# Moving the first block's output projection behind its feed-forward stage, in a time-mix and GELU kernel

## The chip, the cores and the metric

The kernel runs on one core of a Trainium2 chip. The time of a run is the device time of that core in microseconds (us), from the start of the program to its end; the figure for a kernel is the median over runs. A profile of one execution stands beside it: its span runs from the first to the last instruction recorded, a little less than that execution's own time.

## The reference

The input x has 4 sequences of 1024 tokens with 512 channels. Each token is normalized, and the result goes into two branches whose outputs are added to x. The first is a time-mix: a key and a receptance product with 704 hidden units, a decaying running sum over time, and a projection back to 512 channels that is normalized again. The second is a feed-forward network (FFN) with 2048 hidden units, whose activations are rounded to 16 bits.

```python
xn = layernorm(x)
xx = shift(xn) - xn                      # the token before, minus the token
k = (xn + xx * mix_k) @ Wk.T             # 512 -> 704
r = (xn + xx * mix_r) @ Wr.T
state_t = state_{t-1} * exp(-exp(decay)) + relu(k_t)
a = layernorm((state * r) @ Wv.T) * gamma + beta      # 704 -> 512
D = gelu(f16(xn) @ W0.T + bias0).astype(f16)          # 512 -> 2048
E = (D @ W1.T + bias1).astype(f16)                    # 2048 -> 512
out = x + a + E
```

## The kernel before

**Blocks and stages.** The 4096 tokens are cut into 8 blocks of 512 (128 tokens x 4 make a block's token tiles). One loop runs over the blocks. For each block the tensor engine (PE) does, in this order in most blocks: the FFN (`ffn`), the output projection of the time-mix (`attention_out`, tiles po), and the key and receptance products of the next block (`attention`, tiles pk and pr). The 704 hidden units are five chunks of 128 and a half chunk of 64; the half chunk is computed by `half_chunk` (tiles pkr), which splits the PE's array into quarters of 64x64. Its sum `kr` is made on the vector engine (DVE, lines 438 and 439), its relu on the scalar engine (ACT, line 384), its running sum on DVE (line 386) and its product gh on DVE (line 442).

**Where the output projection stands.** In blocks 1 to 6, `attention_out` follows the FFN, and the next block's `half_chunk` is called from inside it (`amid`), right after the 64-row products of the projection (tile gh, line 470). In block 0 and in the last block (`within`), `attention_out` is put into the FFN at step n = 0, and the next block's half chunk then stands alone, behind its five full chunks.

**The FFN.** It has 16 chunks n of 128 hidden units. `up(n)` is eight products with W0, which is kept in a high and a low part (w0h, w0l)[...]; ACT applies the GELU (line 540), DVE casts the result to d (line 542). `down(n)` is eight products of d with the two parts of W1 (line 548). The order on PE is up(0), up(1), and then up(n + 2), down(n) for each n, so down(n) comes five eight-product groups after up(n), less at the end, where no further up stands between.

**Weights in block 0.** W0 and W1 arrive as plain 32-bit tiles `raw`, of which there are three buffers, shared by W0 (`load_w0`, 16 loads of 256 KB in four groups of four) and W1 (`load_w1`, 16 loads). Each is split: ACT copies the rounded high part (line 134), DVE subtracts to get the low part (line 135). A W1 chunk has one of three w1 buffers; in block 0 it is also stored to memory (w1d), from where the later blocks load both parts. up(0) to up(3) read W0's first group, up(12) to up(15) its last. In the kernel before, all four W0 groups are loaded before the FFN of block 0 is written down.

**What orders the work.** Each engine, and SyncE (SP), which issues nearly all DMAs, works through its own list in order. The lists are made ahead of time by a planner: the instruction written first in the program has the higher priority, and an instruction that is ready by the planner's own costs may fill a hole earlier. `tc.issue_after(ins)` puts the instructions in its block that run on the same engine as `ins` behind it in that engine's list. Buffers of one tag are taken in the order of the program. The layernorm of the next block (`next_norm`), its transposes (`transposed`, 16 on DVE, line 216) and its mixing (`mixed_inputs`, lines 349 to 367) are called inside the FFN, at n = 4 and, in block 0, n = 9; tile st6, with two buffers, is shared by the statistics of both layernorms.

Of the kernel before, what the change touches and what calls it, by code (L numbers as in the profile page):

```python
# [1 line left out]

# [9 lines left out]
AF = mybir.ActivationFunctionType  # L12
# [7 lines left out]
def time_mix_and_gelu_ffn(  # L20
# [26 lines left out]
    nc = tc.nc  # L47
# [5 lines left out]
    NC = C // P  # L53
# [79 lines left out]
    def split(hi, lo, raw):  # L133
        nc.scalar.copy(hi, raw)
        nc.vector.tensor_sub(lo, raw, hi.bitcast(F32))
# [4 lines left out]

    w1_dram = [dram.tile([P, 2, C], F32R, name=f"w1d_{n}") for n in range(NN)]

    def load_w0(g):
        for c in range(NC):
            raw = three.tile([P, W0G], F32, tag="raw", name=f"w0raw_{g}_{c}")
            cols = slice(g * W0G, (g + 1) * W0G)
            nc.sync.dma_start(raw, w0T[c * P : (c + 1) * P, cols])
            split(w0h[c][:, cols], w0l[c][:, cols], raw)

    def load_w1(i, n):  # L150
        if i == len(blocks) - 1 and n == NN - 1:

            parts = [
                three.tile([P, C], F32R, tag="raw", name=f"w1_{i}_{n}_{p}") for p in range(2)
            ]
            for p in range(2):
                nc.sync.dma_start(parts[p].bitcast(F32), w1_dram[n][:, p, :].bitcast(F32))
            return parts
        w1 = wide.tile([P, 2, C], F32R, tag="w1", name=f"w1_{i}_{n}", bufs=3)
        if i == 0:  # L160
            raw = three.tile([P, C], F32, tag="raw", name=f"w1raw_{n}")
            nc.sync.dma_start(raw, w1T[n * P : (n + 1) * P, :])
            split(w1[:, 0, :], w1[:, 1, :], raw)
            kept = nc.sync.dma_start(w1_dram[n].bitcast(F32), w1.bitcast(F32))
            if n == NN - 1:
                state["kept"] = kept
        else:
            nc.sync.dma_start(w1.bitcast(F32), w1_dram[n].bitcast(F32))
        return [w1[:, p, :] for p in range(2)]
# [206 lines left out]
    def attention(i, xk, pks=()):  # L376

        b, t0 = blocks[i]  # L380

        def states(h, hw, pk):
            rk = two.tile([P, TB], F32, tag="rk", name=f"rk_{i}_{h}", bufs=1)
            nc.scalar.activation(rk[:hw], pk, AF.Relu)  # L384
            st = two.tile([P, TB], F32, tag="st", name=f"st_{i}_{h}")
            nc.vector.tensor_tensor_scan(  # L386
                st[:hw],
                w_sb[:hw, h : h + 1].to_broadcast([hw, TB]),
                rk[:hw],
                0.0 if t0 == 0 else carry[:hw, h : h + 1],  # L390
                ALU.mult,
                ALU.add,
            )
            if t0 + TB < T:
                nc.gpsimd.tensor_copy(carry[:hw, h : h + 1], st[:hw, TB - 1 : TB])
            return st

        def full_chunks():
            g = one.tile([P, NF, TB], F32, tag="g", name=f"g_{i}")
            for h in range(NF):  # L400
                cols = slice(h * P, (h + 1) * P)
                if h < len(pks):
                    pk = pks[h]
                else:
                    pk = ps_mm.tile([P, TB], F32, tag="mm", name=f"pk_{i}_{h}")
                    for c in range(NC):
                        product(pk, wk_sb, cols, xk[:, c, :], c)
                st = states(h, P, pk)
                pr = ps_mm.tile([P, TB], F32, tag="mm", name=f"pr_{i}_{h}")
                for c in range(NC):  # L410
                    state["pr"] = product(pr, wr_sb, cols, xnT[:, c, 1:], c)
                nc.vector.tensor_mul(g[:, h, :], st, pr)  # L412
            return g

        def tokens(ap, odd):
            return ap.rearrange("p (s two t) -> p s two t", two=2, t=P)[:, :, odd, :]

        def half_chunk():
            gh = one.tile([P, NS // 2, P], F32, tag="gh", name=f"gh_{i}")


            sums = [ps_e.tile([P, TB], F32, tag="pe", name=f"pkr_{i}_{q}") for q in range(2)]
            for c in range(NC):
                for q, sum_ in enumerate(sums):
                    rows = slice(q * HF, (q + 1) * HF)
                    for out_, w, src in (
                        (sum_[:HF], wk_sb, xk[rows, c, :]),
                        (sum_[HF:], wr_sb, xnT[rows, c, 1:]),
                    ):
                        nc.tensor.matmul(  # L430
                            out_,
                            w[c][rows, H0:],
                            src,
                            start=(c == 0),
                            stop=(c == NC - 1),
                        )
            both = two.tile([P, TB], F32, tag="xx", name=f"kr_{i}")
            nc.vector.tensor_copy(both, sums[0])
            nc.vector.tensor_add(both, both, sums[1])  # L439
            st = states(NF, HF, both[:HF])  # L440
            for odd in range(2):
                nc.vector.tensor_mul(
                    gh[odd * HF : (odd + 1) * HF],
                    tokens(st[:HF], odd),
                    tokens(both[HF:], odd),
                )
            return gh

        return full_chunks, half_chunk
# [72 lines left out]
    def ffn(i, xf, between, state):  # L522
# [4 lines left out]
        def up(n):  # L527
            pd = ps_mm.tile([P, TB], F32, tag="mm", name=f"pd_{i}_{n}")
            cols = slice(n * P, (n + 1) * P)
            for c in range(NC):  # L530
                for w in (w0h, w0l):
                    nc.tensor.matmul(  # L532
                        pd,
                        w[c][:, cols],
                        xf[:, c, :],
                        start=(c == 0 and w is w0h),
                        stop=(c == NC - 1 and w is w0l),
                    )
            d16 = two.tile([P, TB], F16, tag="d16", name=f"d16_{i}_{n}")
            state["gelu"] = nc.scalar.activation(d16, pd, AF.Gelu, bias=b0_sb[:, n : n + 1])  # L540
            d = wide.tile([P, TB], F32R, tag="d", name=f"d_{i}_{n}", bufs=4)
            nc.vector.tensor_copy(d, d16)  # L542
            return d

        def down(n, s, d, w1, first=0, end=NN, sum_=None, cols=slice(0, C)):
# [27 lines left out]
        AHEAD = 2  # L573
        waiting = [(up(n), load_w1(i, n)) for n in range(AHEAD)]
        for n in range(NN):
            if n in between:
                between[n]()
            if n + AHEAD < NN:
                waiting.append((up(n + AHEAD), load_w1(i, n + AHEAD)))
            if n < NN - last:  # L580
                operands = waiting.pop(0)
                for s in range(NS):
                    down(n, s, *operands, end=NN - last if s in by_columns else NN)
# [19 lines left out]
    first_x16s, xk, pks = first_inputs(x_now, behind)  # L603

    full_chunks, half_chunk = attention(0, xk, pks)
    g = full_chunks()
    xf = ffn_input(0, first_x16s())
# [2 lines left out]
    for i in range(len(blocks)):  # L612
        more = i + 1 < len(blocks)
        if i == 0:
            for grp in range(N // W0G):
                load_w0(grp)
            behind.close()
            load_late_constants()
        if more:

            with tc.issue_after(state["kept"].ins) if i == 1 else nullcontext():
                x_now = load_x(i + 1)

        def out_stage():
            state["zs"] = attention_out(i, g, gh)

        def next_norm():
            with tc.issue_after(added.ins) if added else nullcontext():
                layernorm(i + 1, x_now)

        def next_inputs():
            transposed(x_now)
            state["mixed"] = mixed_inputs(i + 1, state["gelu"])

        within = i == 0 or not more
        added = state.get("added")
        between = {0: out_stage} if within else {}
        if more:
            between[4] = next_norm
            between[9 if i == 0 else 7] = next_inputs  # L640
        pe = ffn(i, xf, between, state)
        if more:
            x16s, xk = state["mixed"]
            e16s = [rounded(i, s, pe[s]) for s in range(NS)]
            xf = ffn_input(i + 1, x16s)
            full_chunks, half_chunk = attention(i + 1, xk)
            next_gh = []
            if within:
                zs = state["zs"]
            else:  # L650
                zs = attention_out(i, g, gh, lambda: next_gh.append(half_chunk()))
            for s in range(NS):
                finish(i, s, zs[s], e16s[s])
            g = full_chunks()
            gh = next_gh[0] if next_gh else half_chunk()
# [43 lines left out]
```

## Time and profile before

| quantity | value |
|---|---|
| median of 3 runs | 937.12 us (936.71 to 937.28) |
| profiled execution, its own time | 937.08 us |
| its span | 935.2 us |
| PE busy | 930.0 us, 99% |
| DVE busy | 501.6 us, 54% |
| ACT busy | 164.4 us, 18% |
| TensorE clock granted | 1.0 of full speed |

The profile's page has a row of busy shares for each engine, the chain of work that ended last, and the costliest groups of instructions. "PE" is the matmuls, "PEld" the loading of their stationary operand. A 32-bit product is recorded as two matmuls, a product of rounded operands as one; "pk L222 x8" is therefore one chunk of four products. Times in the chain are start and length in us, from the span's start.

### The profile page before, as it was taken

The numbers are of one execution on the slowest core, as the hardware profiler recorded it, in microseconds if no ns is written. First come the engines' busy times: TensorE is split into PE (matmuls) and PEld (weight loads), VectorE is DVE, ScalarE is ACT, GpSimd is POOL, SyncE is SP. The second block draws the span as 40 slices with busy tenths as digits, with TensorE's granted clock in tenths as the row PEclk, the third lists the DMA queues.
The fourth block names the chain that finished last, engine by engine and source line by source line (L and its number), as shares of the span: only waits on it lengthen the run. The fifth ranks groups of instructions, "written<-read, shape, count | busy, mean of one in ns | idle before, by whom it ended". The sixth has DMA issues, their size and how long they took to land.

```text
span 935.2 us, 9363 instructions
## 1 busy us (share of the span) xinstructions
PE 930.0 (99%) x3521; PEld 593.8 (63%) x3521; DVE 501.6 (54%) x878; ACT 164.4 (18%) x273; POOL 55.6 (6%) x130
## 2 busy tenths in 40 slices
PE   9999999999999999999999999999999999999998
PEld 8448854886448854588545885458844588445687
DVE  6678772833846338463484535755357552552513
ACT  5423410220002200112001220112200121001011
POOL 1110000000100001000010000100001000000100
PEclk9999999999999999999999999999999999999999
DMA  9654660343204432054320543105431044310243
GB/s 305 203 168 158 225 224 1 132 161 113 90 0 158 142 107 90 0 166 150 100 80 0 180 142 116 59 1 187 150 113 46 12 146 139 109 45 1 67 150 121
DMA packets 40728, 106.53 MB, mean 114 GB/s; under 512 B 4559, under 2 KB 6636, under 8 KB 40684
## 3 DMA queue, kind: packets, MB, share of 16 engines
q1 hardware_dynamic: 40624, 105.92, 34.3%
q8 instruction: 28, 0.46, 0.2%
q14 instruction: 16, 0.13, 0.0%
q10 hardware_dynamic: 60, 0.02, 0.0%
HBM read 89.14 MB, written 16.78 MB: 113 GB/s over the span
## 4 chain that ended last, share of the span: by engine, by line
PE 99%; DVE 0%; DMA 0%; SPq 0%; issue 0%
PE pd L532 25%; PE pe L548 24%; PE po L459 15%; PE pk L222 15%; PE pr L222 15%; PE pkr L430 3%; PE po L470 2%; DMA wk<-in_L_attn_Wk 0%; DVE z L516 0%; PE pt L261 0%; DVE e L566 0%; SPq L86 0%; DVE e L511 0%; PE idle L243 0%; SPq L97 0%
## 5 line engine op out<-in xcount | busy, mean ns | idle before, releaser
L548 PE MATMUL pe<-w,d 128*128 128x512 f32 x1008 | 246.7, 389 | 0.0
L548 PEld LDWEIGHTS pe<-w,d 128*128 128x128 f32 x1008 | 189.2, 188 | 39.4 <-DVE d L542 0.3
L532 PE MATMUL pd<-xf,w0h 128*128 128x512 f32 x512 | 202.9, 396 | 0.0
L532 PE MATMUL pd<-xf,w0l 128*128 128x512 f32 x512 | 199.6, 390 | 0.0
L542 DVE CAST d<-d 128x512 fp32r<-128x512 f16 x128 | 54.3, 425 | 185.3 <-ACT d L540 183.9
L540 ACT ACTIVATE d<-pd,small_sb 128x512 f16<-128x512 f32 x128 | 87.8, 687 | 345.9 <-PE pd L532 345.9
L222 PE MATMUL pk<-xk,wk 128*128 128x512 f32 (+1 forms) x392 | 144.8, 516 | 0.1
L222 PE MATMUL pr<-xnT,wr 128*128 128x512 f32 x320 | 143.7, 592 | 0.0
L459 PE MATMUL po<-wv_sb,g 128*128 128x512 f32 x320 | 140.8, 595 | 0.0
L222 PEld LDWEIGHTS pk<-xk,wk 128*128 128x128 f32 x392 | 67.6, 191 | 70.7 <-issue 70.2
L532 PEld LDWEIGHTS pd<-xf,w0h 128*128 128x128 f32 x512 | 96.2, 188 | 23.1 <-issue 2.7
L532 PEld LDWEIGHTS pd<-xf,w0l 128*128 128x128 f32 x512 | 96.1, 188 | 21.8 <-issue 1.9
L222 PEld LDWEIGHTS pr<-xnT,wr 128*128 128x128 f32 x320 | 60.6, 190 | 76.3 <-issue 75.9
L459 PEld LDWEIGHTS po<-wv_sb,g 128*128 128x128 f32 x320 | 60.2, 190 | 75.9 <-issue 75.3
L216 DVE STREAM_TRANSPOSE xnT<-x 32x512 f32<-32x512 f32 x112 | 78.7, 702 | 2.0
L384 ACT ACTIVATE rk<-pk 128x512 f32<-128x512 f32 x40 | 23.9, 597 | 229.9 <-PE pk L222 229.5
L195 DVE BATCH_NORM_STATS2 sty<-po 128x6 f32<-128x512 f32 x32 | 22.0, 688 | 62.3 <-PE po L470 60.7
L386 DVE TENSOR_TENSOR_SCAN st<-small_sb,carry,rk 128x512 f32<-128x512 f32 (+1 forms) x24 | 30.7, 1280 | 42.0 <-ACT rk L384 42.0
L412 DVE TENSOR_TENSOR g<-st,pr 128x512 f32<-128x512 f32 x40 | 27.3, 683 | 35.4 <-PE pr L222 34.7
L386 DVE TENSOR_TENSOR_SCAN st<-small_sb,rk 128x512 f32<-128x512 f32 (+1 forms) x24 | 29.2, 1218 | 29.2 <-ACT rk L384 29.2
L189 POOL TENSOR_SCALAR ry<-mvy 128x1 f32<-128x1 f32 x32 | 11.4, 356 | 433.2 <-DVE mvy L196 433.2
L384 ACT ACTIVATE rk<-kr 64x512 f32<-64x512 f32 x8 | 5.0, 630 | 146.4 <-DVE kr L439 146.4
(69 smaller groups left out, 494.0 us busy)
## 6 DMA issues: line engine op xcount, KB each, us to landing
w<-w1d SPq DMA_DIRECT2D x111, 512.0 KB, 3.3
x<-in_L_attn_x SPq DMA_DIRECT2D x32, 256.0 KB, 3.5
xres<-in_L_attn_x SPq DMA_DIRECT2D x32, 256.0 KB, 2.7
w1d<-w SPq DMA_DIRECT2D x16, 512.0 KB, 2.9
out<-z SPq DMA_DIRECT2D x28, 256.0 KB, 2.6
w0raw<-in_L_ffn_W SPq DMA_DIRECT2D x16, 256.0 KB, 3.7
w1raw<-in_L_ffn_W SPq DMA_DIRECT2D x16, 256.0 KB, 3.4
wr<-in_L_attn_Wr SPq DMA_DIRECT2D x4, 352.0 KB, 5.5
```

The source lines that it names most:

```text
L195: nc.vector.bn_stats(st6, src)
L216: nc.vector.transpose(dst[i * Q : (i + 1) * Q, :, :, j, :], src[j * Q : (j + 1) * Q, :, :, i, :],)
L222: return nc.tensor.matmul(dst, w[c][:, cols], src, start=(c == 0), stop=(c == NC - 1))
L384: nc.scalar.activation(rk[:hw], pk, AF.Relu)
L386: nc.vector.tensor_tensor_scan(st[:hw], w_sb[:hw, h : h + 1].to_broadcast([hw, TB]), rk[:hw], 0.0 if t0 == 0 else carry[:hw, h : h + 1], A ...
L412: nc.vector.tensor_mul(g[:, h, :], st, pr)
L430: nc.tensor.matmul(out_, w[c][rows, H0:], src, start=(c == 0), stop=(c == NC - 1),)
L459: nc.tensor.matmul(pos[s], g[:, h, s * P : (s + 1) * P], wv_sb[:, h, :], start=(first and h == 0), stop=(not first and h == NF - 1),)
L532: nc.tensor.matmul(pd, w[c][:, cols], xf[:, c, :], start=(c == 0 and w is w0h), stop=(c == NC - 1 and w is w0l),)
L540: state["gelu"] = nc.scalar.activation(d16, pd, AF.Gelu, bias=b0_sb[:, n : n + 1])
L542: nc.vector.tensor_copy(d, d16)
L548: nc.tensor.matmul(pe[s] if sum_ is None else sum_, d[:, s * P : (s + 1) * P], w1[part][:, cols], start=(n == first and part == 0), stop=( ...
```

## The change

Block 0 is treated as blocks 1 to 6: its output projection comes behind its FFN, and the half chunk of block 1 is called from inside it. Around this, three orders are set for block 0. The splits of W1 on ACT are put behind the GELU of the same chunk (for n = 0, behind the half chunk's relu), and on DVE behind the sum `kr`. The last group of W0 is loaded inside the FFN, one tile at n = 2, 4, 6 and 8, its ACT copies behind the newest GELU. The transposes of block 1 are put behind the cast of chunk 1. `between` becomes a list of calls for each n.

```diff
-    def load_w0(g):
-        for c in range(NC):
+    def load_w0(g, chunks=range(NC)):
+        for c in chunks:
...
-            split(w1[:, 0, :], w1[:, 1, :], raw)
+            behind = state["gelu" if n else "relu"]
+            with tc.issue_after(behind.ins), tc.issue_after(state["kr"].ins):
+                split(w1[:, 0, :], w1[:, 1, :], raw)
...
-            nc.scalar.activation(rk[:hw], pk, AF.Relu)
+            state["relu"] = nc.scalar.activation(rk[:hw], pk, AF.Relu)
...
-            nc.vector.tensor_add(both, both, sums[1])
+            state["kr"] = nc.vector.tensor_add(both, both, sums[1])
...
-            nc.vector.tensor_copy(d, d16)
+            state["cast", n] = nc.vector.tensor_copy(d, d16)
...
-            if n in between:
-                between[n]()
+            for put in between[n]:
+                put()
...
-            for grp in range(N // W0G):
+            for grp in range(N // W0G - 1):
                 load_w0(grp)
...
+        def last_w0(c):
+            with tc.issue_after(state["gelu"].ins):
+                load_w0(N // W0G - 1, [c])
+
...
-            transposed(x_now)
+            with tc.issue_after(state["cast", 1].ins) if i == 0 else nullcontext():
+                transposed(x_now)
             state["mixed"] = mixed_inputs(i + 1, state["gelu"])
 
-        within = i == 0 or not more
+        within = not more
         added = state.get("added")
-        between = {0: out_stage} if within else {}
+        between = [[] for _ in range(NN)]
+        if within:
+            between[0].append(out_stage)
+        if i == 0:
+            for c in range(NC):
+                between[2 + 2 * c].append(partial(last_w0, c))
         if more:
-            between[4] = next_norm
-            between[9 if i == 0 else 7] = next_inputs
+            between[4].append(next_norm)
+            between[9 if i == 0 else 7].append(next_inputs)
```

More of the change, by code (lines that the diff above doesn't have):

```diff
@@ L1 @@
 from contextlib import ExitStack, nullcontext
+from functools import partial
 import concourse.bass as bass
```

## The prediction

> **What bounds the kernel now.** I read the page's busy rows and its chain shares first.
>
> ```profile
> PE 930.0 (99%) x3521; PEld 593.8 (63%) x3521; DVE 501.6 (54%) x878; ACT 164.4 (18%) x273; POOL 55.6 (6%) x130
> PE 99%; DVE 0%; DMA 0%; SPq 0%; issue 0%
> ```
>
> PE is the bound over the whole span, with 5.2 us not busy, at the two ends. So a change that leaves the matmuls as they are gains only what PE loses between them. I therefore took the chain in order of time, windowed on block 0 and on a later block, and compared starts.
>
> ```profile
> 44.13 3.60 PE pkr L430 x32
> 47.73 3.87 PE pd L532 x16
> 51.60 8.58 PE po L459 x20
> 60.18 1.88 PE po L470 x16
> 62.06 8.78 PE po L459 x20
> 70.84 1.84 PE pd L532 x8
> ...
> 159.62 3.60 PE pkr L430 x32
> 163.21 5.67 PE pd L532 x24
> ```
> ```profile
> 278.50 5.48 PE pd L532 x24
> ...
> 347.02 3.44 PE pkr L430 x32
> ...
> 393.60 5.48 PE pd L532 x24
> ```
>
> The pieces join without holes. A block, from the first pd to the next block's, takes 115.48 us for block 0 (47.73 to 163.21), 115.29 for block 1 (163.21 to 278.50) and 115.10 for each later one. The half chunk shows why: alone it takes 3.60, inside the projection 3.44, and the three ups behind it take 5.67 in place of 5.48. Next, DVE and ACT around the start of FFN 0:
>
> ```profile
> 54.52 0.68 DVE L438 COPY kr<-pkr 128x512 f32<-128x512 f32 x1
> 56.09 0.63 ACT L384 ACTIVATE rk<-kr 64x512 f32<-64x512 f32 x1 [2.21 <-DVE kr L439]
> 56.73 1.28 ACT L540 ACT_TABLE_LOAD   x1
> 58.03 1.27 ACT L540 ACTIVATE d<-pd,small_sb 128x512 f16<-128x512 f32 x2
> ```
>
> pkr is finished at 47.73, but kr starts 6.8 us later, behind splits of W0 and W1 that wait for DMAs. Nothing is lost, because the 19.2 us of po cover it.
>
> [...] Here the spacing agrees with the busy row: eight matmuls in 1.81 us, throughout. [...] The load is 1.28 here, and the GELU starts 0.02 after it, the load 0.01 after the relu; I use the trace.
>
> **Part 1, the projection moved.** No matmul is added or removed. Block 0 still starts behind a lone half chunk (+0.19), so it takes 115.10 + 0.19 = 115.29; block 1 then starts like block 2 and takes 115.10. Sum 230.39 against 230.77: **-0.38 us**. The evacuation of po (statistics, POOL's rstd, z, four xres loads) goes where blocks 1 to 6 have it, without a PE hole there. On SP the four xres issues at 65.5 to 75.6 move past FFN 0; they keep two buffers and have its length to land.
>
> **Part 2, the start of FFN 0.** The cover of 19.2 us is gone: down(0) is wanted at 47.73 + 5.67 = 53.40. Its chain, from rows above: kr can start at 47.76 (in block 1 it starts 0.03 after pkr), relu 1.57 later (56.09 - 54.52) at 49.33, GELU 0 another 1.94 later (58.03 - 56.09) at 51.27. One GELU is 0.69, so 51.96; the cast, 0.43, ends at 52.4. If W1's copy (0.62) follows that GELU, it ends at 52.58 and its subtraction (0.69) at 53.27; the low part is needed by the second matmul, at 53.63. If the copy goes ahead of the GELU, the cast ends at about 53.0. The margin is 0.3 us either way, on condition that DVE is free at 47.76. It should be: W0's twelfth subtraction ran at 43.42, the four behind it leave for the FFN, W1's are put behind kr, and only the scan (1.22) and product (0.68) of chunk 4 remain, with 3.6 us for them. The bounds are 0 and the 6.1 us that a repeat of the old kr delay would give (GELU 0 at 58.03, cast done by 59.5, less 53.40). I take **+0.2 us**, an estimate for handoffs that this sum lacks.
>
> **Part 3, W1's splits behind the GELU.** With T the end of up(n), a GELU starts 0.2 later (up(2) ends 72.5, GELU 72.72). The split is ready at T + 0.2 + 0.69 + 0.62 + 0.69 = T + 2.2, plus any DVE backlog. down(n) starts at T + 5 x 1.81 = T + 9.1; at n = 15, T + 3.63. So backlog costs nothing below **6.9 us** (1.4 at n = 15). Behind the waiting copy on ACT stand the next GELU and, on SP, the store of w1d and the next raw loads behind it. A raw load lands 3.4 us after issue and the ring of three turned over in 1.7 us a tile during W0; the FFN wants 20 tiles in 58 us, 2.9 each. Hidden, cost 0.
>
> **Part 4, W0's last quarter.** Four loads, four copies (0.62) and four subtractions (0.69) move from 44 to 50 us to about 57 to 86. The last copy follows GELU 9; up(12) comes five groups after up(9) ends, so the margin is like that of part 3. PE needs nothing else; cost 0, but DVE gets 2.8 us more in the FFN.
>
> **Part 5, DVE's load.** The cover for parts 3 and 4 is DVE keeping up. Before, it did not quite:
>
> ```profile
> 95.22 0.43 DVE L542 CAST d<-d 128x512 fp32r<-128x512 f16 x1
> ...
> 99.62 0.42 DVE L542 CAST d<-d 128x512 fp32r<-128x512 f16 x1
> ```
>
> The GELU for the second cast started at 94.48 and ended at 95.17, so the cast was 4.45 us late. The lag grew by some 0.7 us a chunk (1.7, 2.05, 3.2, 3.7, 4.45) while transposes filled every hole, and was gone two chunks later. After: 16 casts 6.9, 16 + 4 subtractions 13.8, the kr chain 3.5, transposes 11.2, mixing 8.7, layernorm 5.6 make 49.7 us, for 52.8 us from 47.73 to the end of up(15). The layernorm can go earlier: its st6 no longer waits behind the projection's statistics (stx followed the last sty at once, at 71.49, though x was asked for by 23.3), and DVE waited 8.9 us for W0 copies between 24 and 48. That leaves 44.1 of 52.8. The filler is 16 transposes, W0's 2.8 us and two mixing pairs (2.8): 16.8 us where before it was 14.0 over five chunks, so six chunks at 0.7, **a lag of about 4.2 us**, under 6.9. The bounds are 0 and the slow rival's 3.3.
>
> **Sum.** 937.08 - 0.38 + 0.2 = 936.9; the median shown stands 0.04 above the profiled execution, which changes nothing. The other edits (the list of calls, the transposes behind cast 1, which is past by then) cost nothing in PE's list.
>
> **Rivals.** (a) *Slower: DVE's backlog makes W1's low parts late.* The place is down(4) to down(9) of block 0, where PE has no other work. If the layernorm stays inside, the filler is 22.4 us, eight chunks; at the steepest growth seen, 1.15 a chunk, the lag reaches 9.2, less 6.9 gives 2.3. W0 tiles in the ring can add a landing, about 1 us more: +3.3, thus 940.0. For it: the 4.45 us already seen. Against it: the hole for the layernorm. It decides at a lag of 6.9 us, and is over 0.2% from 9.2. (b) *Slower at down(0).* Something with a DMA or POOL behind it is still ahead of kr on DVE; past 3.6 us of free time plus 0.3 each us costs one. At +2.5, 939.2. For it: this happened before; against it: the splits that did it are moved away. (c) *The saving is not made*, because the planner keeps the half chunk alone or PE's list changes: 937.1. (d) *Faster by over 0.2%* would need PE time that isn't there: 0.38 is all that the views show.
>
> **Chances.** The forecast 0.62, (c) and small stalls under 1.9 us 0.12, (a) 0.15, (b) 0.08, (d) 0.03. About 0.2%, 1.9 us, is what a measurement of this kernel can tell from no change. So faster 0.03, same 0.74, slower 0.23. The range goes from 936.4 (the whole saving and a little of the run's spread) to 940.0, the end of (a).
>
> **What would show it.** Right: pd x24 at 47.73 for 5.67 us and pe at 53.4; po x20 behind FFN 0 at about 105.9 with pkr x32 of 3.44 inside; first pd of block 1 near 163.0 to 163.2, of block 2 near 278.3; PE busy time unchanged. Wrong: a hole in PE ahead of down(0) with DVE or ACT as releaser (b), or ahead of a later down or up(12) with line 135 as releaser (a); statistics of block 1 still behind 50 us would speak for (a). A shift of over 1 us anywhere after block 1 would refute the whole reading.

## The result, and the profile after

The changed kernel takes **938.81 us** (median of 14 runs, 937.96 to 942.35) against 937.00 for the kernel before (14 runs, 936.53 to 937.61): ratio 1.0025, interval 1.0018 to 1.0033. It is slower by about 1.8 us, where 936.9 and no measurable change were forecast. Its profiled execution is the longest of the 14, 942.35 us (span 940.6); what differed between two executions is shown below. I therefore account for the profile by itself, 5.27 us above the profiled execution of before, and for the median afterwards.

First the page after: the busy row, the shares of the chain, and the group of `down`.

```profile
PE 931.8 (99%) x3521; PEld 595.0 (63%) x3521; DVE 502.2 (53%) x878; ACT 162.9 (17%) x273; POOL 54.5 (6%) x130
PE 95%; DVE 2%; DMA 1%; issue 1%; ACT 0%; POOL 0%; DVEq 0%; POOLq 0%; SPq 0%; ACTq 0%
L551 PE MATMUL pe<-w,d 128*128 128x512 f32 x1008 | 248.0, 391 | 3.9 <-DVE d L545 3.9
```

The number of matmuls is the same, 3521. PE's share of the chain fell from 99% to 95%: at one place the chain leaves PE. The third row names it, an idle of 3.9 us ahead of a `down`, ended by the cast to d. PE is also busy 1.8 us longer for the same instructions; that is a second loss. The chain of waits after, in order of time (start and length in us):

```profile
21.47 5.46 DMA x<-in_L_attn_x
...
44.13 4.33 DMA w0raw<-in_L_ffn_W
48.48 0.63 ACT w0h L135
49.13 0.69 DVE w0l L136
49.82 1.14 DVE st L389
51.06 0.69 DVE g L415
51.75 0.61 DVE kr L441
...
56.78 0.44 DVE d L545
57.26 3.30 PE pe L551 x8
```

Read upwards: down(0) starts at 57.26, behind the cast, behind `kr`, which DVE reaches at 51.7 though pkr was finished at about 47.6. Ahead of `kr` on DVE stand scan and product of chunk 4 and a W0 subtraction at 49.13 whose raw tile came late. At the head of the whole chain is the DMA of x. DVE's timeline shows where that enters (in brackets: idle before, and what ended it):

```profile
26.96 0.69 DVE L198 BATCH_NORM_STATS2 stx<-x 128x6 f32<-128x512 f32 x1 [3.49 <-DMA x<-in_L_attn_x]
27.57 0.67 DVE L415 TENSOR_TENSOR g<-st,pr 128x512 f32<-128x512 f32 x1
28.16 1.22 DVE L389 TENSOR_TENSOR_SCAN st<-small_sb,rk 128x512 f32<-128x512 f32 x1
...
49.13 0.69 DVE L136 TENSOR_TENSOR w0l<-w0raw,w0h 128x512 fp32r<-128x512 f32 x1 [1.50 <-ACT w0h L135]
```

Scan 1 and W0's twelfth subtraction in the profile before, for comparison:

```profile
23.47 1.22 DVE L386 TENSOR_TENSOR_SCAN st<-small_sb,rk 128x512 f32<-128x512 f32 x1
...
43.42 0.68 DVE L135 TENSOR_TENSOR w0l<-w0raw,w0h 128x512 fp32r<-128x512 f32 x1
```

The first statistic of block 1's layernorm, stx, now stands in DVE's list ahead of scan 1. Before, st6's two buffers held it behind the projection's statistics, until 71.49; with the projection moved behind the FFN, nothing holds it, and the planner put it here. Its x was asked for at 21.47 and lands at 26.96, so DVE does nothing for 3.49 us, and all that stands behind it waits too: the scan that ran at 23.47 before runs at 28.16, the three raw buffers come free later, and W0's twelfth subtraction, at 43.42 before, runs at 49.13. It is 5.7 us late. Before, 3.6 us lay between its end and that of pkr, of which the scan and product of chunk 4 need 1.9 (1.22 and 0.68), so 1.7 us were to spare: `kr` is late by 5.7 - 1.7 = 4.0 us.

The second loss is the clock. By stretches (columns: length; busy time of PE, PEld, DVE, ACT, POOL, with counts; granted clock; DMA share; GB/s):

```profile
54.43:57.84 3.41, 0.58 (x3) 0.49 (x4) 3.24 (x7) 3.40 (x5) 0.57 (x1) 1.00 0.38 137
57.84:61.26 3.42, 3.42 (x10) 2.65 (x9) 3.31 (x7) 0.71 (x2) 0.00 (x0) 0.50 0.68 247
```

The granted clock is 1.00 in the first row and 0.50 in the second: after the hole PE runs at half clock, from 57.84 to 61.26 us, 3.41 us in the clock's records, and loses half of it, 1.7 us. The drop didn't come inside the hole: PE had resumed 0.58 us before it.

**The profile adds up, but for 0.2 us:** 3.93 (hole) + 1.71 (half clock) - 0.38 (the half chunk moved inside) = 5.26 us. From the first matmul of pkr of block 0 to that of block 2 the kernel takes 193.15 us after and 187.68 before, 5.47 more. (That the whole execution is 5.27 longer, so near the sum, is chance: this one's pkr also started 0.08 us earlier.) The other 0.2 us fit a slow restart: where a down waits for its cast, its weight load waits too (4.35 us here), and in experiments 1, 2, 3 and 9, where down(0) starts within about 0.1 us of the end of its cast, it takes 2.06 to 2.11 us in place of 1.81. The end of FFN 0 shows the half chunk in place: it takes 3.44 inside the projection.

```profile
111.75 8.58 PE po L462 x20
120.33 1.88 PE po L473 x16
122.21 3.44 PE pkr L433 x32
```

### The profile page after: what moved, and what is told of

Read it like the earlier page. It is cut to its first block, busy times and chain, and to the rows that moved or that the text cites. A ratio compares the mean times of both kernels' runs of the same rounds, so it can differ in the third digit from the quotient of the medians.

```text
span 940.6 us, 9382 instructions
## 1 busy us (share of the span) xinstructions
PE 931.8 (99%) x3521; PEld 595.0 (63%) x3521; DVE 502.2 (53%) x878; ACT 162.9 (17%) x273; POOL 54.5 (6%) x130
## 4 chain that ended last, share of the span: by engine, by line
PE 95%; DVE 2%; DMA 1%; issue 1%; ACT 0%; POOL 0%; DVEq 0%; POOLq 0%; SPq 0%; ACTq 0%
PE pe L551 24%; PE pd L535 24%; PE po L462 15%; PE pk L225 14%; PE pr L225 13%; PE pkr L433 3%; PE po L473 2%; DMA w0raw<-in_L_ffn_W 1%; DMA x<-in_L_attn_x 1%; PE idle L246 1%; DVE w0l L136 0%; DVE st L389 0%; DVE z L519 0%; PE pt L264 0%; DVE e L569 0%
```

## The experiments

Each time is the median beside runs of the kernel before on the same chip: 937.15 (33 runs) for the first four, 937.25 (24 runs) for the next four, 937.10 (29 runs) for the last two.

**1. The statistic without its wait.** Two theories: A, stx waits for x at the head of DVE's list; B, the layernorm's work ahead of `kr` is too much for DVE. The changed kernel is taken, and the first statistic reads a weight tile that is already there, at the same place in the list.

```diff
-            stats_of(mv, s, xs[:, s, :], f"stx_{i}_{s}")
+            at_hand = i == 1 and s == 0
+            with tc.issue_after(state["scan"].ins) if at_hand else nullcontext():
+                stats_of(mv, s, wk_sb[0][:, :C] if at_hand else xs[:, s, :], f"stx_{i}_{s}")
...
-            nc.vector.tensor_tensor_scan(
+            scan = nc.vector.tensor_tensor_scan(
...
+            state.setdefault("scan", scan)
```

> The changed kernel with one source replaced: the first of the four statistics of block 1's layernorm reads a weight tile (wk) that has long been in place, not x of block 1, so block 1's output is computed with one wrong mean and variance. Every engine's list is otherwise that of the changed kernel. Theory A (the wait for x's DMA, 3.49 us at the head of DVE's list, pushes back the splits of W0 and so kr): DVE starts scan 1 at about 23.5 in place of 28.2, W0's twelfth subtraction is back near 45 to 46, the hole ahead of down(0) is under 1 us, 936.7 to 937.3. Theory B (the layernorm's own 5.6 us of DVE work ahead of kr is the delay, wait or not): the hole stays at 2 us or more, 938.5 to 939. Theory C (the loss is made later in the FFN by DVE's backlog): no change, 938.8.

Measured: **936.78 us** (936.30 to 937.18, 13 runs), ratio 0.9995, interval 0.9987 to 1.0003. DVE's timeline of this kernel:

```profile
23.27 0.69 DVE L198 BATCH_NORM_STATS2 stx<-wk 128x6 f32<-128x512 f32 x1
...
44.12 0.69 DVE L136 TENSOR_TENSOR w0l<-w0raw,w0h 128x512 fp32r<-128x512 f32 x1 [0.51 <-ACT w0h L135]
...
47.56 0.69 DVE L444 COPY kr<-pkr 128x512 f32<-128x512 f32 x1 [0.82 <-PE pkr L436]
```

The statistic starts 3.7 us earlier, the twelfth subtraction is back at 44.12, and `kr` waits for PE again, not PE for `kr`. The whole layernorm is still ahead of `kr`, and there is no hole at down(0), which starts at 53.21. So it is A; B's work costs PE nothing here, though it takes up slack: DVE waits 0.82 us for pkr, where it waits 2.78 in experiment 2.

**2. The layernorm behind cast 1.** The remedy: one order more, which keeps the layernorm out of DVE's list until the FFN has started.

```diff
-            with tc.issue_after(added.ins) if added else nullcontext():
+            with tc.issue_after(added.ins if added else state["cast", 1].ins):
                 layernorm(i + 1, x_now)
```

> The changed kernel with the whole layernorm of block 1 put behind the cast of chunk 1 on DVE. Theory A and theory B: DVE's list up to kr is that of the kernel before without the fourth W0 group; kr near 47.8, down(0) within 0.5 us of 53.4, and the 0.38 us of the half chunk is seen: 936.6 to 937.0. Theory C, which is rival (a) of the prediction (22.4 us of filler inside the FFN): holes ahead of down(4) to down(11), 938 to 940.

Measured: **936.70 us** (936.49 to 937.05, 13 runs), ratio 0.9995, interval 0.9987 to 1.0004. This is the shortest of all the kernels; the interval includes no change, so that it beats the kernel before is not established, though its median lies 0.45 us lower. Its chain has no hole, and its DVE timeline shows the start of the FFN nearly as the prediction had laid it out:

```profile
43.94 3.60 PE pkr L433 x32
47.53 5.68 PE pd L535 x24
53.22 2.06 PE pe L551 x8
55.28 1.81 PE pd L535 x8
```
```profile
47.56 0.69 DVE L441 COPY kr<-pkr 128x512 f32<-128x512 f32 x1 [2.78 <-PE pkr L433]
...
52.69 0.76 DVE L545 CAST d<-d 128x512 fp32r<-128x512 f16 x2
```

The first cast ends at 53.1 and down(0) starts at 53.22, but the cast is not quite hidden. The d that it writes is what PE loads as weights, and in the profile before, the load for a down starts 0.22 us ahead of its first matmul (79.55 and 79.77). Here 0.1 us lay between cast and matmul, and down(0) takes 2.06 us, not 1.81. So 0.25 of the 0.38 us is lost again. From the first pkr of block 0 to that of block 2 this profile is only 0.09 us shorter than the one before; its span also starts 0.19 us better, which the change doesn't explain. It also bears on rival (a), since here the layernorm is wholly inside the FFN. The cast of chunk 8 starts at 80.31 although its GELU ended at 75.95, a lag of 4.4 us, the largest in this profile; no later down waited for it.

**3. The layernorm behind `kr`, not behind the cast.** The same line with `state["kr"].ins`.

> The changed kernel with the layernorm of block 1 put behind kr on DVE, three instructions ahead of the place of e6. In DVE's list two statistics (0.65 us each) then stand between kr and the half chunk's scan, W1's first subtraction and the cast of chunk 0. Theory A and B: these 1.3 us and a little more eat the 0.3 us of margin, hole ahead of down(0) of 0.7 to 1.2 us, 937.4 to 937.9. Theory C: as e6, 938 to 940.

Measured: **937.98 us** (937.62 to 938.35, 13 runs), ratio 1.0008, interval 1.0000 to 1.0016, just above the band expected, but the hole at down(0) is less than half of what I expected. There are two holes, both small. Two statistics (1.28 us) slip between `kr` and the half chunk's scan, so the first cast comes at 53.40 and PE waits 0.3 us at down(0). The second, on PE's weight loads at down(11), is rival (a) in small, a W1 subtraction that is late behind other DVE work:

```profile
94.31 1.46 PEld L551 LDWEIGHTS pe<-w,d 128*128 128x128 f32 x7 [0.35 <-DVE w L136]
```

The two make 0.65 of the 1.0 us by which its span exceeds that of experiment 2; the other 0.35 is a later start (pkr at 44.29 against 43.94). So there is no margin at down(0), and 1.28 us of statistics in the wrong place show. The lag of the cast reaches 5.2 us here, at chunk 7.

**4. Without the order on the W1 splits.** From the changed kernel:

```diff
-            behind = state["gelu" if n else "relu"]
-            with tc.issue_after(behind.ins), tc.issue_after(state["kr"].ins):
-                split(w1[:, 0, :], w1[:, 1, :], raw)
+            split(w1[:, 0, :], w1[:, 1, :], raw)
```

> The changed kernel without the order on W1's splits (they may go ahead of the half chunk's sum and relu, as in the kernel before). Three W1 splits, each waiting for its load, then stand ahead of kr. Theory A and B: kr only at about 55, GELU 0 at about 58.5, hole ahead of down(0) of 6 to 7 us and about 2 us of slow matmuls after it as in the profile of the changed kernel: 944 to 946. If the order on W1 does not matter for kr: 938.8.

Measured: **943.24 us** (942.75 to 943.67, 5 runs), ratio 1.0065, interval 1.0052 to 1.0077. Slower as expected, but the size was missed: `kr` ran at 52.80, the hole is 4.6 us, and the clock was halved for 3.41 us (57.41 to 60.82).

**5. The kernel before, with the layernorms' statistics set free.** Each use of st6 gets buffers of its own, so block 1's statistics no longer queue behind the projection's.

```diff
-        st6 = two.tile([P, 6], F32, tag="st6", name=name)
+        st6 = two.tile([P, 6], F32, tag=name[:3], name=name)
```

> The kernel before with one edit: the statistics tiles get a tag for each of their two uses, so that those of block 1's layernorm need not wait for those of the projection. The planner then puts the layernorm ahead of scan 1, as in the changed kernel, and DVE should wait 3 to 3.5 us for x there. Theory A with the cover: the 19.2 us of po between up(1) and up(2) hide a later kr (about 58 in place of 54.5), 936.9 to 937.5, or up to 2 us more if the third po tile waits for the PSUM bank that GELU 0 frees. Without the cover's help (the wait costs PE by itself, through pk and pr): 939 or more.

Measured: **946.36 us** (946.12 to 946.57, 4 runs), ratio 1.0099, interval 1.0084 to 1.0114. The same wait appears without any of the change (DVE's timeline), and PE loses time behind it (PE's waits: line waited for, us in total, times, longest):

```profile
26.32 0.69 DVE L195 BATCH_NORM_STATS2 stx<-x 128x6 f32<-128x512 f32 x1 [3.04 <-DMA x<-in_L_attn_x]
```
```profile
PE po L470 <- DVE gh L442: 4.5, 1, 4.5
PE pd L532 <- DVE mvy L196: 1.3, 1, 1.3
PE pe L548 <- DVE d L542: 0.3, 1, 0.3
```

`kr` came at 58.64 instead of 54.52, and the half products (po, line 470) waited 4.5 us for gh. Not all of that is the wait: block 1's transposes, which no order holds back in the kernel before, were set free as well. Four of them (0.70 each) now run between `kr` and gh, which takes 6.2 us from one to the other in place of 4.4, and eleven more run ahead of the projection's statistics, whose lateness makes the 1.3 us. The clock was still full at 62.0, was halved by 63.0 and stayed so until about 69.64; PE was busy for the last 5.2 us of this, so 2.6 were lost. Holes and clock make 4.5 + 1.3 + 0.3 + 2.6 = 8.7 of the 9.45 us by which the stretch from the first pkr to that of block 2 is longer; the rest is about 0.25 a hole, as in the slow restarts above. This refutes a sentence of my prediction. The late `kr` of before was not covered by 19.2 us of po: gh ended at 58.94 and was wanted at 60.18, so the cover was 1.2 us. And it shows what the ring of two buffers had done all along: it kept stx, and the transposes after it, behind `kr`.

**6. All of W0 ahead of the FFN, as before.** From the changed kernel, the last group goes back in front of `ffn(0)` (`range(N // W0G)`, no `last_w0`).

> The changed kernel with all four W0 groups loaded before the FFN, as in the kernel before. Four more W0 splits, one per 1.7 us of the ring, then stand ahead of kr. Theory A: kr at about 56, hole ahead of down(0) of 7 to 8 us and 1.7 us for a halved clock after it, 945 to 947. If the last quarter's place is of no account: 938.8.

Measured: **945.09 us** (944.41 to 945.95, 4 runs), ratio 1.0085, interval 1.0068 to 1.0102, in the band expected, but by luck: the hole at down(0) grew to 6.2 us, not to 7 or 8, and the half clock to 6.83 us (57.60 to 64.43), not 3.4. PE was busy for 4.8 of these, so the clock lost 2.4 us. From the first matmul of down(0) to the next up it took 3.58 us (59.63 to 63.21), against 1.81 in experiment 10, at full clock.

**7 and 8. A hole of a set size.** The kernel of experiment 2, with the GELU of block 0's chunk 0 done 4 and 7 times, to see whether the clock is halved after holes of 2.4 and 4.1 us (the diff has 3 more; 6 more in the other).

```diff
+            for _ in range(3 if i == 0 and n == 0 else 0):
+                nc.scalar.activation(d16, pd, AF.Gelu, bias=b0_sb[:, n : n + 1])
             state["gelu"] = nc.scalar.activation(d16, pd, AF.Gelu, bias=b0_sb[:, n : n + 1])
```

> e6 with GELU 0 of block 0 done four times in place of once (same result), to set the hole ahead of down(0) by itself. The last of the four starts about 54.4, so down(0) starts near 55.6 in place of 53.2: a hole of 2.4 us. If a hole costs its own length: 939.1. If the clock is halved after it as after the 3.93 us hole of the changed kernel's profile: 940.8.

> As g3_hole, with seven GELUs: down(0) near 57.3, a hole of 4.1 us. If a hole costs its own length: 940.8. If the clock is halved for some 3.3 us after it, which loses 1.7 us: 942.5.

Measured: 938.09 us (20 runs, ratio 1.0009, interval 1.0002 to 1.0016) and 940.08 us (5 runs, 1.0034, 1.0021 to 1.0047). Neither has the hole that it was built for, so they say nothing of the clock after holes of such lengths. The planner saw the longer GELU and put further ups ahead of down(0), so the holes were 0.7 us in sum in one and 1.2, 0.7 and 0.6 in the other, and the clock stayed full in both profiles (1.00 in every stretch from 53 to 68 us).

**9. The changed kernel once more**, for another profile.

> The changed kernel once more, since its first profile was of one of its longest executions (942.35) while most took 938.5 to 939.1. Theory A: the wait of DVE for x ahead of scan 1 is there in every execution, 2.5 to 3.5 us. An execution near 938.7 has a hole ahead of down(0) of about 2 us (938.7 less 936.7 of e6) and no halved clock after it; one near 941 to 942 has 3 to 4 us and a halved clock for 3.4 us, which costs 1.7.

Measured: **939.45 us** (937.71 to 943.20, 17 runs), ratio 1.0027, interval 1.0019 to 1.0035. The profiled execution took 938.96, near the first median. DVE's timeline and PE's wait at down(0) in it:

```profile
25.91 0.69 DVE L198 BATCH_NORM_STATS2 stx<-x 128x6 f32<-128x512 f32 x1 [2.56 <-DMA x<-in_L_attn_x]
...
49.89 0.68 DVE L441 COPY kr<-pkr 128x512 f32<-128x512 f32 x1
```
```profile
PE pe L551 <- DVE d L545: 2.3, 1, 2.3
```

x landed about a microsecond sooner, the hole is 2.3 us, and the clock was not halved (mean 1.000). Hole and half chunk make 2.27 - 0.38 = 1.9 us; with 0.3 for the slow restart (down(0) takes 2.11) this is the 2.2 us by which the stretch from the first pkr to that of block 2 is longer. The execution began 0.2 us better and is 1.9 us above that of before, as is the median of the 14 (1.8). Between the two profiles the cost differs with the landing of x and W0, and in some executions the half clock seems to be added: the executions with a mean clock of 0.999 or 1.000 took 937.7 to 939.5 us, those with 0.996 to 0.998 took 940.0 to 943.2.

**10. Experiment 2 without the order on the W1 splits.**

> e6 (layernorm behind the cast of chunk 1) without the order on W1's splits. W0's splits are then as early as in e6, but three W1 splits stand ahead of kr on DVE and the half chunk's relu on ACT. Theory A: kr near 50 in place of 47.6, GELU 0 near 53.5, hole ahead of down(0) of 1.2 to 2 us, 937.9 to 938.7. If only the layernorm's wait made kr late: 936.7, and the order on W1 would be needless.

Measured: **937.13 us** (936.73 to 941.14, 13 runs), ratio 1.0007, interval 0.9998 to 1.0015. The hole that I expected at down(0) isn't there: in the profiled execution (936.82 us) `kr` starts at 47.68 and down(0) at 53.32.

```profile
53.32 1.81 PE pe L549 x8
```

With the layernorm out of the way, W1's raw tiles had landed in time for three splits ahead of `kr`. None then stands between `kr` and the first cast, which starts at 52.22, 0.47 us earlier than in experiment 2; down(0) has no slow restart, and this profile shows the whole saving: 0.37 us from the first pkr to that of block 2. But 4 of the 13 runs took 938.2 to 941.1, where experiment 2 has none over 937.05. That the order guards against late loads is what this suggests; no profile of such a run was taken.

## Why the prediction was wrong, step by step

- **What bounds it, and part 1: right.** Blocks 0 and 1 now start as counted, and the -0.38 is seen whole where nothing else is lost: -0.37 in experiment 10's profile.
- **Part 2: its chain was nearly right, its condition failed.** With DVE free, experiments 1 and 2 start `kr` at 47.56, GELU 0 at 51.59, and down(0) at 53.2. In experiment 2, W1's first split went ahead of the GELU; for that order I had the cast done at 53.0, and it was done at 53.1, from a `kr` 0.2 earlier. So the chain is 0.3 longer than its rows gave, and I had left out that d is wanted by the weight load, 0.22 before the matmul in the profile before. There was no margin: down(0) lost 0.25 us, about the +0.2 that I had added for handoffs. What failed is "on condition that DVE is free at 47.76. It should be: W0's twelfth subtraction ran at 43.42". I carried that time over from the trace of before, though the same prediction moved the layernorm ahead of it.
- **Part 5: the step that failed.** "The layernorm can go earlier", I wrote, and counted it as relief: 5.6 us of work into 8.9 us of DVE's waits. I had read that its x was asked for by 23.3, but not when it lands, nor at which place in DVE's list the planner would put the statistics, and ahead of what. The work does fit, as experiment 1 shows. The wait that came with it, 3.49 us ahead of scan 1, doesn't: it moved W0's twelfth subtraction by 5.7 us and opened a hole of 3.93 us at down(0), 2.3 in experiment 9. While DVE waited for x, nothing that stood behind stx in its list ran: scan 1 came at 28.16, not at 23.47.
- **Rival (b) is what happened.** I gave it 0.08. Its mechanism fits, a DMA ahead of `kr`, and its 939.2 stands beside 938.81 and 939.45. That number was in part luck: it counted 3.6 us as free on DVE, of which 1.9 were needed for chunk 4, and it named no size for the wait. I weighed against it that the splits which had delayed `kr` were moved away; a new instruction took their place.
- **Parts 3 and 4: right as far as tried.** With the order of experiment 2 W0's last quarter didn't hold PE up, nor did W1's splits beyond the 0.25 us at down(0). Experiment 6 shows that W0's last quarter does matter, for `kr`: back in front, the hole is 6.2 us. Experiment 4 says the same of W1's order while the layernorm is early, experiment 10 shows no clear gain from the order once the layernorm is late: medians of 937.13 without and 936.70 with it, taken on two chips, with intervals that overlap.
- **Rival (a) didn't come.** With the layernorm inside the FFN I had reckoned a lag of 9.2 us; 4.4 was seen in experiment 2 and 5.2 in experiment 3, under the 6.9 that PE needs. With the layernorm early, as the forecast had it, the lag is 3.9 in experiment 9, against 4.2 forecast. Growth at the steepest step seen, carried through eight chunks, was too much. Its mechanism cost 0.35 us in experiment 3.
- **Left out of the sum: the clock.** A hole in PE can cost more than its length: 1.7 us on top of 3.93, 2.4 on top of 6.2.

What stays open is which holes are followed by half clock. The profiles have one of 2.3 us without and one of 3.9 us with it; experiments 7 and 8 were to fill the gap and didn't.

## What to carry to other kernels

An instruction that a change sets free costs not only its duration: put earlier into an in-order list, it makes everything behind it in that list wait for its own input, here 3.49 us. So for each order that a change dissolves, a shared ring of buffers among them, ask what may now move up, when its data land, and who stands behind it; then give it a place by an explicit order, as experiment 2 does with one line. And read a cover from the consumer that is wanted first (here gh, 1.2 us), not from the length of the work beside it (19.2 us).

## What the hardware showed that I had not expected

Half clock came with the long holes around the start of FFN 0 and not with the short ones (times in us from the span's start):

| profile | holes in PE | half clock |
|---|---|---|
| changed kernel | 3.93, to 57.26 | 57.84 to 61.26 |
| experiment 4 | 4.6, to 57.81 | 57.41 to 60.82 |
| experiment 5 | 4.5, to 64.44; then 1.3 and 0.3 | from between 62.0 and 63.0 to 69.64 |
| experiment 6 | 6.2, to 59.63 | 57.60 to 64.43 |
| experiment 7 | 0.7 in sum | none |
| experiment 8 | 1.2, 0.7 and 0.6 | none |
| experiment 9 | 2.3, to 55.48 | none |

It lasted 3.41 us in the first two, 6.83 in experiment 6. It began 0.58 us behind the hole in the changed kernel's profile and inside the hole in experiments 4 to 6. What decides when the clock is halved, and for how long, was not shown. The same program ran with half clock in one profile (942.35 us) and without it in another (938.96); DVE's wait for x ended at 26.96 in the first and at 25.91 in the second, and the holes were 3.93 and 2.3 us.

Executions of the changed kernel spread over 5.5 us (937.71 to 943.20), where those of experiment 2 spread over 0.56.
